# Messages' second pass of a graph layer: source rows gathered by index for seven of nine slot tiles

## The chip, the cores and the metric

The kernel runs on one core of a Trainium2 chip. A core has five engines that work side by side, each through its own queue in order: TensorE (PE, matrix products into PSUM; its weight loads are shown as PEld), VectorE (DVE), ScalarE (ACT), GpSimd (POOL) and SyncE (SP). DMAs move data between memory (HBM) and the on-chip SBUF. SP and ACT issue plain DMAs, POOL issues indirect ones, which take a list of row numbers. The metric is the device time of one execution in microseconds (us), median of several.

## The reference, cut to what matters

Four graph layers, each followed by a mixture of experts, are applied to 3125 nodes of 256 features with 50000 edges. The change lies in the second graph layer:

```python
def _L1_gnn_ref(h, edge_indices, edge_attr, W1, b1, W2, b2, W_ih, b_ih, W_hh, b_hh):
    src, dst = edge_indices
    m_in = concatenate([h[src], h[dst], edge_attr], -1)   # 256 + 256 + 64
    msg = relu(m_in @ W1.T + b1) @ W2.T + b2
    agg = segment_sum(msg, src, N)                          # sums by SOURCE node
    return gru_cell(agg, h, W_ih, b_ih, W_hh, b_hh)
```

(Written here in short.) With W1 cut in three by its input, an edge's hidden row is relu(P[src] + Q[dst] + edge_attr W1c), where P = h W1a + b1 and Q = h W1b are tables with one row per node. The kernel sums the relu rows by source and multiplies by W2 afterwards, once per node, with a count of edges for b2.

## The kernel before, in words

Nodes lie in 25 tiles of 128 and in seven blocks: six of four tiles and one of one tile. `mpnn_buckets` works in two passes over the edges.

**Pass one** (from L1298) takes the 392 edge tiles of 128 edges in order of destination, 28 groups of 14. `prepare` (L1275) finishes a block of nodes from the layer before: it fetches expert results, adds, normalizes, transposes on PE and multiplies by W1b into the table `q_tab` in HBM, two tiles at a time, copied by ACT and written by SP. It is called when the next group's destinations reach a new block. Each group forms Q[dst] + edge_attr W1c by one product per tile (L1316), out of a few `q_tab` rows near the destination (`near_load`, issued by SP), ACT copies it to `mq_r`, a last column holds the source's place in its tile (L1311), and POOL scatters the 128 rows of each tile by index into `slot_r` (L603). `slot_r` has a bucket for each tile of source nodes, 18 slot tiles of 128 rows long (8 for the last).

**Pass two** (from L1320) walks the buckets. For each bucket, `mb_p` is P for its 128 nodes (products L1344, b1 added at L1346), cut into three bf16 parts whose sum is exact enough (`split3`). For each group of GB = 9 slot tiles: SP loads `r` (`mb_r`, 1.16 MB, three buffers); DVE makes the mask `eq` per tile from the last column (L1360); PE transposes the masks (L1365) and ACT casts them to bf16 (`hot`, L1366); PE multiplies `hot` with the three parts (L1372), which places P[src] at each edge's row; DVE adds `r` (L1373), ACT applies relu (L1374) into `f` (`mb_m`, two buffers); and PE sums rows by source with the mask (L1376) into `acc`. After the four buckets of a block, `block` is the GRU cell (L984 and around), and `router.block` of the block before stands after the first bucket.

Tiles come from pools with a number of buffers; a buffer is free again when the last reader is done. The order of each engine's queue is laid down before the run by a planner: it walks the program with times of its own, takes of the instructions whose inputs it believes ready the one that stands first in the program, and so pulls later work forward where it sees an engine idle, as far as buffers allow. At run time each queue is strictly in order.

Of the kernel before, what the change touches and what calls it, by code (L numbers as in the profile page):

```python
# [8 lines left out]
F32 = mybir.dt.float32  # L9
# [8 lines left out]
P = 128  # L18
N = 3125
D = 256  # L20
# [75 lines left out]
def gnn_ffn_kernel(ctx: ExitStack, tc: tile.TileContext, I: dict, out: bass.AP):  # L96
# [1157 lines left out]
        def tile(self, shape, dtype, name):  # L1254
            return self.pool.tile(shape, dtype, name=self.name)

    def mpnn_buckets(pos, slot_r, collect, weights, router):

        with tc.tile_pool(name="mq", bufs=1) as p, tc.tile_pool(name="mq_t", bufs=1) as tp, \
                tc.tile_pool(name="mq_ps", bufs=2, space=PSUM) as pbt:
            q_tab = tc.dram_tile([NR, D], F32, name="mq_q")
            lane = p.tile([P, 1], F32, name="mq_l")
            V.tensor_scalar(lane, node_id[:, 0:1], 64.0, None, op0=OP.subtract)

            near = [p.tile([P, len(QUADS), D], F32, name=f"mq_n{k}") for k in range(4)]
            for t in near:
                for k in range(len(QUADS)):
                    nc.scalar.dma_start(t[:64, k], I["L1_gnn_W1T_c"])  # L1270
            w1b = load_w(p, "L1_gnn_W1T_b")
            add = add_two(x, weights)

            def prepare(s, n):
                t0, nt = s // P, n // P  # L1275
                for u0 in range(0, nt, 2):
                    m = min(2, nt - u0)
                    g = collect(tp, t0 + u0, m, 2)
                    for u in range(m):
                        add(t0 + u0 + u, g[:, :, u])  # L1280
                norm_tiles(tp, x, xn, t0, nt)
                xT = block_transposed(tp, pbt, xn, t0, nt, "mq_xT")
                for t in range(0, nt, 2):
                    m = min(2, nt - t)
                    pt = pbt.tile([P, 512], F32, name="bt_p")
                    for v in range(m):
                        for c in range(2):
                            PE.matmul(pt[:, v * D:(v + 1) * D], xT[:, c, (t + v) * P:(t + v + 1) * P], w1b[:, c],
                                      start=c == 0, stop=c == 1)
                    pv = pt[:, :m * D].rearrange("p (t d) -> p t d", d=D)  # L1290
                    o = tp.tile([P, 2, D], F32, name="mq_o", bufs=2)[:, :m]
                    S.copy(o, pv)
                    nc.sync.dma_start(node_rows(q_tab)[:, t0 + t:t0 + t + m], o)

            blocks = list(BLOCKS)
            put = scatter(slot_r, ET)
            with tc.tile_pool(name="mq_e", bufs=2) as ep, tc.tile_pool(name="mq_p", bufs=4, space=PSUM) as ps:
                for g in range(ET // GF):  # L1298
                    ahead = W_TO[min(g + 1, ET // GF - 1)]
                    while blocks and blocks[0][0] < ahead * P:  # L1300
                        prepare(*blocks.pop(0))

                    ea = ep.tile([P, GF * P], F32, name="mq_ea")
                    nc.sync.dma_start(ea[:64], I["edge_attrT"][:, g * GF * P:(g + 1) * GF * P])
                    row = ep.tile([P, GF * P], BF16, name="n_row")
                    nc.sync.dma_start(row[64:], near_row[g:g + 1].to_broadcast([64, GF * P]))
                    V.tensor_scalar(ea[64:], row[64:], lane[64:], None, op0=OP.is_equal)
                    for k in range(len(QUADS)):
                        near_load(g, k, near[g % 4][64:, k], q_tab, 1)
                    r = ep.tile([P, GF, D + 1], F32, name="mq_r", bufs=3)  # L1310
                    V.tensor_copy(r[:, :, D], sloc[:, g * GF:(g + 1) * GF])  # L1311
                    for u in range(0, GF, 2):
                        pt = ps.tile([P, 2, D], F32, name="mq_pe")
                        for v in range(2):
                            i = g * GF + u + v
                            PE.matmul(pt[:, v], ea[:, (u + v) * P:(u + v + 1) * P], near[g % 4][:, (u + v) // 4],  # L1316
                                      start=True, stop=True)
                        S.copy(r[:, u:u + 2, :D], pt)
                        for v in range(2):
                            i = g * GF + u + v  # L1320
                            put(pos[:, i:i + 1], r[:, u + v])
        with tc.tile_pool(name="mb", bufs=1) as p, tc.tile_pool(name="mb_e", bufs=2) as ep, \
# [3 lines left out]
                tc.tile_pool(name="mb_pp", bufs=2, space=PSUM) as ppp, \  # L1326
                tc.tile_pool(name="gru_ps", bufs=2, space=PSUM) as gps, \
                tc.tile_pool(name="gru_pt", bufs=1, space=PSUM) as gpt:
            w1a = load_w(p, "L1_gnn_W1T_a")
            b1 = load_bc(p, "L1_gnn_b1", D)  # L1330
            block, routed = gru(p), []
            for s, n in BLOCKS:
                hT = bp.tile([P, 2, 512], F32, name="mb_hT")
                for c in range(2):
# [4 lines left out]
                seg = bp.tile([P, 4, W], F32, name="mb_seg")  # L1339
                for u in range(n // P):  # L1340
                    b = s // P + u
                    pp = ppp.tile([P, 2, D], F32, name="mb_pp")
                    for c in range(2):
                        PE.matmul(pp[:, 0], hT[:, c, u * P:(u + 1) * P], w1a[:, c], start=c == 0, stop=c == 1)  # L1344
                    po = bp.tile([P, D], F32, name="mb_p")
                    V.tensor_tensor(po, pp[:, 0], b1, op=OP.add)  # L1346
                    parts = bp.tile([P, 3, D], BF16, name="mb_parts")
                    split3(bp, parts.unsqueeze(1), po.unsqueeze(1))
                    acc = pacc.tile([P, 512], F32, name="mb_acc")
                    for k0 in range(0, B_TILES[b], GB):  # L1350
                        m = min(GB, B_TILES[b] - k0)
                        r = ep.tile([P, GB, D + 1], F32, name="mb_r", bufs=3)
                        row = (b * BT + k0) * P
                        nc.sync.dma_start(r[:, :m], slot_r[row:row + m * P].rearrange("(k p) w -> p k w", p=P))
                        eq = ep.tile([P, GB, P], F32, name="mb_eq")
                        hot = ep.tile([P, GB, P], BF16, name="mb_hot")
                        f = ep.tile([P, GB, W], F32, name="mb_m")
                        V.memset(f[:, :m, D:], 1.0)
                        for k in range(m):
                            V.tensor_scalar(eq[:, k], iota1, r[:, k, D:], None, op0=OP.is_equal)  # L1360
                        for h0 in range(0, m, 4):
                            h1 = min(h0 + 4, m)
                            pt = ppt.tile([P, 512], F32, name="mb_tp")
                            for k in range(h0, h1):
                                PE.transpose(pt[:, (k - h0) * P:(k - h0 + 1) * P], eq[:, k], ident)  # L1365
                            S.copy(hot[:, h0:h1], pt[:, :(h1 - h0) * P].rearrange("p (k j) -> p k j", j=P))  # L1366
                        for h0 in range(0, m, 2):
                            h1 = min(h0 + 2, m)
                            pp = ppp.tile([P, 2, D], F32, name="mb_pp")
                            for k in range(h0, h1):  # L1370
                                for z in range(3):
                                    PE.matmul(pp[:, k - h0], hot[:, k], parts[:, z], start=z == 0, stop=z == 2)  # L1372
                            V.tensor_tensor(f[:, h0:h1, :D], r[:, h0:h1, :D], pp[:, :h1 - h0], op=OP.add)  # L1373
                            S.activation(f[:, h0:h1, :D], f[:, h0:h1, :D], AF.Relu)  # L1374
                        for k in range(m):
                            PE.matmul(acc[:, :W], eq[:, k], f[:, k], start=k0 + k == 0, stop=k0 + k == B_TILES[b] - 1)  # L1376
                    S.copy(seg[:, u], acc[:, :W])
                    if routed:
                        router.block(gp, Shared(gp, "segT"), Shared(gpt, "gru_t"), *routed.pop())
# [873 lines left out]
    with tc.If(in_windows == 1) as branch:  # L2253
        slot_r = tc.dram_tile([B_ROWS + 2 * P, D + 1], F32, name="slot_r")
        hy_sums = tc.dram_tile([NR + P, D + 1], F32, name="hy_sums")
        with tc.tile_pool(name="m1", bufs=1) as rp:
            router = Router(rp, 32, 1, "L1_ffn_router_wT", "L1_ffn_router_b")
            with tc.tile_pool(name="bk", bufs=1) as p:
                pos = p.tile([P, ET], I32, name="bk_i")
                with tc.tile_pool(name="m0", bufs=1) as mp:  # L2260
                    with tc.tile_pool(name="bk_t", bufs=1) as tp:
                        collect, weights = gat_gelu(mp, slot_r, hy_sums, bucket_slots(tp, pos))
                    mpnn_buckets(pos, slot_r, collect, weights, router)
            collect = top1_experts(router.hot)
        h_tab = tc.dram_tile([NR, D], F32, name="hc_tabc1")
        hyper_bn(h_tab, hy_sums, collect)
# [105 lines left out]
```

## Time and profile before

| what | value |
|---|---|
| median of the runs | 5283.61 us (5283.53 to 5300.94, 3 runs) |
| profiled execution | 5289.04 us, its span 5287.3 us |
| pass one, first to last scatter on POOL | 901 to 1445 us |
| pass two, from the first load of `r` to the last block's GRU | 1447 to about 2165 us |
| PE / DVE / ACT / POOL busy over the span | 73% / 46% / 23% / 43% |

The profile is one execution. "Busy" leaves out waits and the issuing of DMAs. A group row gives line, engine, operation, output<-inputs, shape, count, then busy us, mean ns of one, and idle time before it with what ended it. A timeline row begins with start and length in us. Matmul records of one fp32 product come in pairs, so counts at such lines are twice the products.

### The profile page before, as it was taken

The numbers are of one execution on the slowest core, as the hardware profiler recorded it, in microseconds if no ns is written. First come the engines' busy times: TensorE is split into PE (matmuls) and PEld (weight loads), VectorE is DVE, ScalarE is ACT, GpSimd is POOL, SyncE is SP. The second block draws the span as 40 slices with busy tenths as digits, with TensorE's granted clock in tenths as the row PEclk, the third lists the DMA queues.
The fourth block names the chain that finished last, engine by engine and source line by source line (L and its number), as shares of the span: only waits on it lengthen the run. The fifth ranks groups of instructions, "written<-read, shape, count | busy, mean of one in ns | idle before, by whom it ended". The sixth has DMA issues, their size and how long they took to land. (4 is left out here: it accounts for less than half of the span.)

```text
span 5287.3 us, 55222 instructions
## 1 busy us (share of the span) xinstructions
PE 3846.2 (73%) x16260; PEld 2652.4 (50%) x16260; DVE 2432.2 (46%) x9200; ACT 1239.1 (23%) x2517; POOL 2296.0 (43%) x2426
## 2 busy tenths in 40 slices
PE   4687647545399999445788888888888788875794
PEld 3466536434266666323555545556454444543583
DVE  6687746111055555456666556542333213336224
ACT  2010112212133333122344344343000200002121
POOL 3777454776700000227433343101777447771421
PEclk7788778767699999676888888888788668885797
DMA  6955256545432321265533443213333223331463
GB/s 195 296 157 157 91 180 211 162 154 160 146 100 86 91 90 62 64 201 145 139 99 106 115 114 96 56 51 114 105 105 105 68 81 104 105 105 32 167 216 131
DMA packets 391473, 655.82 MB, mean 124 GB/s; under 512 B 58519, under 2 KB 298330, under 8 KB 386810
## 3 DMA queue, kind: packets, MB, share of 16 engines
q1 hardware_dynamic: 266352, 339.40, 21.1%
q0 software_dynamic: 113712, 305.42, 19.4%
q10 hardware_dynamic: 11098, 7.31, 0.5%
q8 instruction: 140, 2.29, 0.2%
q14 instruction: 171, 1.40, 0.1%
HBM read 505.27 MB, written 146.64 MB: 123 GB/s over the span
## 5 line engine op out<-in xcount | busy, mean ns | idle before, releaser
L264 POOL DMA_INDIRECT hc_wm<-hc_tabc,src_col x784 | 748.1, 954 | 586.6 <-DMA a_L_gnn_c_b_col<-in_L_gnn_c_b_col 239.9
L348 PE MATMUL w_acc<-hc_wm,w_eq 128*128 128x256 f32 x2208 | 761.4, 474 | 191.7 <-DMA hc_wm<-hc_tabc,src_col 129.5
L348 PEld LDWEIGHTS w_acc<-hc_wm,w_eq 128*128 128x128 f32 x2208 | 447.7, 227 | 505.8 <-DVE w_eq L341 229.6
L341 DVE TENSOR_SCALAR w_eq<-iota,dloc,ew 128x128 f32<-128x128 f32 (+1 forms) x784 | 299.6, 384 | 750.3 <-PE w_acc L348 742.4
L264 POOL DMA_INDIRECT hb_r<-hy_x,src_col x392 | 380.7, 971 | 587.5 <-PE hb_acc L2026 304.3
L603 POOL DMA_INDIRECT slot_x<-xn,sl_i x125 | 121.5, 972 | 963.9 <-issue 832.3
L603 POOL DMA_INDIRECT slot_r<-mq_r,bk_i x392 | 396.2, 1011 | 181.4 <-issue 86.7
L264 POOL DMA_INDIRECT gw_m<-gat_h,src_col x392 | 402.4, 1027 | 133.7 <-issue 121.2
L1174 PE MATMUL gw_acc<-gw_m,gw_eqt 128*128 128x264 f32 x1104 | 310.6, 442 | 120.1 <-issue 87.5
L1316 PE MATMUL mq_pe<-mq_n,mq_ea 128*128 128x256 f32 x784 | 226.6, 460 | 210.6 <-issue 137.1
L1174 PEld LDWEIGHTS gw_acc<-gw_m,gw_eqt 128*128 128x128 f32 x1104 | 235.3, 219 | 182.4 <-issue 92.3
L603 POOL DMA_INDIRECT rows_y<-se_y,se_to x175 | 180.0, 1029 | 320.3 <-DVE se_y L696 186.1
L1316 PEld LDWEIGHTS mq_pe<-mq_n,mq_ea 128*128 128x128 f32 x784 | 183.8, 238 | 253.2 <-issue 198.2
L2026 PE MATMUL hb_acc<-hb_r,hb_eq 128*128 128x257 f32 x784 | 257.5, 459 | 54.3 <-DVE hb_eq L2023 45.9
L2056 PE MATMUL hb_pc<-n_near,n_hot 126*128 126x257 bf16 x392 | 123.9, 325 | 201.8 <-DVE hbe_a L2060 137.8
L1905 ACT ACTIVATE hb_h<-hb_ph,hb_o,hb_s 128x512 f32<-128x512 f32 (+2 forms) x256 | 172.9, 681 | 318.0 <-PE hb_ph L1903 317.7
L2026 PEld LDWEIGHTS hb_acc<-hb_r,hb_eq 128*128 128x128 f32 x784 | 170.7, 232 | 132.5 <-DVE hb_eq L2023 65.9
L683 ACT ACTIVATE se_h<-se_ph,se_w 128x256 f32<-128x256 f32 (+1 forms) x243 | 110.4, 455 | 494.7 <-PE se_ph L680 343.8
L2169 ACT COPY hc_seg<-w_acc 128x256 f32<-128x256 f32 x50 | 18.6, 372 | 874.4 <-PE w_acc L348 846.5
L680 PE MATMUL se_ph<-se_xT,se_w 128*128 128x256 f32 (+1 forms) x972 | 219.1, 370 | 3.7 <-DMA se_w<-in_L_ffn_lanes 1.4
L1903 PE MATMUL hb_ph<-hb_xT,hb_w 128*128 128x512 f32 (+2 forms) x512 | 212.7, 548 | 9.5 <-ACT hb_h L1905 9.1
L689 PE MATMUL se_py<-se_w,se_h 128*128 128x256 f32 x886 | 214.1, 384 | 2.3 <-ACT se_h L683 1.9
(543 smaller groups left out, 7073.9 us busy)
## 6 DMA issues: line engine op xcount, KB each, us to landing
mb_r<-slot_r SPq DMA_DIRECT2D x48, 1156.5 KB
se_w<-in_L_ffn_lanes SPq DMA_DIRECT2D x34, 1026.0 KB
hb_w<-in_L_ffn_W SPq DMA_DIRECT2D x128, 256.0 KB
w_row<-in_dst_row SPq DMA_DIRECT2D x28, 896.0 KB
se_r<-slot_x SPq DMA_DIRECT2D x66, 257.0 KB
se_w<-in_L_ffn_lanes SPq DMA_DIRECT2D x32, 513.0 KB
hb_w<-in_L_ffn_Wo SPq DMA_DIRECT2D x64, 256.0 KB
mq_ea<-in_edge_attrT SPq DMA_DIRECT2D x28, 448.0 KB
```

The lines of the kernel that those rows point to most:

```text
L264: nc.gpsimd.indirect_dma_start(out=dst, out_offset=None, in_=table, in_offset=bass.IndirectOffsetOnAxis(ap=idx, axis=0))
L341: V.tensor_scalar(eq[:, :n], iota256[:, :n], dloc[:, i:i + 1], scale[:, u:u + 1], op0=OP.is_equal, op1=OP.mult)
L348: PE.matmul(acc[t][:, :width], eq[:, k * P:(k + 1) * P], m[:, u, :width], start=i == W_FIRST[t], stop=i == W_LAST[t])
L603: d = nc.gpsimd.indirect_dma_start(out=table, in_=rows, in_offset=None, out_offset=bass.IndirectOffsetOnAxis(ap=idx, axis=0)).ins
L680: PE.matmul(ph, w[:, c, :P] if f < P else w[:, c * f + j * P:c * f + (j + 1) * P], xT[:, c], start=c == 0, stop=c == 1)
L689: PE.matmul(py[:, u], h[:, j, u * P:(u + 1) * P], w[:, :, P:2 * P] if f < P else w[:, o2 + j * D:o2 + (j + 1) * D], start=j == 0, stop=j = ...
L1174: PE.matmul(acc[t][:, :W], eq[:, k * P:(k + 1) * P], m[:, u], start=False, stop=i == W_LAST[t])
L1316: PE.matmul(pt[:, v], ea[:, (u + v) * P:(u + v + 1) * P], near[g % 4][:, (u + v) // 4], start=True, stop=True)
L1903: PE.matmul(ph[:, :n], ws[e, i][:, k, j * P:(j + 1) * P], src[:, k, :n], start=k == 0, stop=k == 1)
L1905: S.activation(o[:, j, :n], ph[:, :n], AF.Relu, bias=shift[i][:, e, j:j + 1], scale=scale[i][:, e, j:j + 1])
L2026: PE.matmul(acc[0][:, :D + 1], eq, b[:, u], start=u == 0, stop=u == GF - 1)
L2056: PE.matmul(pc[:, :D + 1], hot[:, u * P:(u + 1) * P], near[:, u // 4], start=True, stop=True)
```

## The change

`prepare` in pass one also multiplies the block by W1a, DVE adds b1, and SP writes the result into a second table `p_tab` (`mq_p`) in HBM. In pass two, a helper `fetch` loads `r` of a group, turns its last column into row numbers `ix` on DVE (`mb_ix`; place + 128 b - 1, at least 0) and has POOL gather the rows of `p_tab` by index straight into `f` for the first 7 of 9 tiles (6 of 8 in the last group). `fetch` of the next group stands in the program at the head of each group. The masks are still made for all nine tiles. Transposes, `hot` and products with the parts remain for the last two tiles only, which are added and passed through relu first; for the gathered ones DVE adds `r` and `f` in place, two tiles at a time. `mb_p` is read from `p_tab` instead of computed. `f` gets three buffers.

```diff
-    def mpnn_buckets(pos, slot_r, collect, weights, router):
+    def mpnn_buckets(pos, slot_r, collect, weights, router, p_tab):
...
             w1b = load_w(p, "L1_gnn_W1T_b")
+            w1a = load_w(p, "L1_gnn_W1T_a")
+            b1 = load_bc(p, "L1_gnn_b1", D)
...
                 for t in range(0, nt, 2):
                     m = min(2, nt - t)
-                    pt = pbt.tile([P, 512], F32, name="bt_p")
-                    for v in range(m):
-                        for c in range(2):
-                            PE.matmul(pt[:, v * D:(v + 1) * D], xT[:, c, (t + v) * P:(t + v + 1) * P], w1b[:, c],
-                                      start=c == 0, stop=c == 1)
-                    pv = pt[:, :m * D].rearrange("p (t d) -> p t d", d=D)
-                    o = tp.tile([P, 2, D], F32, name="mq_o", bufs=2)[:, :m]
-                    S.copy(o, pv)
-                    nc.sync.dma_start(node_rows(q_tab)[:, t0 + t:t0 + t + m], o)
+                    for w, tab in ((w1b, q_tab), (w1a, p_tab)):
+                        pt = pbt.tile([P, 512], F32, name="bt_p")
+                        for v in range(m):
+                            for c in range(2):
+                                PE.matmul(pt[:, v * D:(v + 1) * D], xT[:, c, (t + v) * P:(t + v + 1) * P], w[:, c],
+                                          start=c == 0, stop=c == 1)
+                        pv = pt[:, :m * D].rearrange("p (t d) -> p t d", d=D)
+                        o = tp.tile([P, 2, D], F32, name="mq_o", bufs=4)[:, :m]
+                        if w is w1b:
+                            S.copy(o, pv)
+                        else:
+                            V.tensor_tensor(o, pv, b1.unsqueeze(1).to_broadcast([P, m, D]), op=OP.add)
+                        nc.sync.dma_start(node_rows(tab)[:, t0 + t:t0 + t + m], o)
...
-            w1a = load_w(p, "L1_gnn_W1T_a")
-            b1 = load_bc(p, "L1_gnn_b1", D)
             block, routed = gru(p), []
+
+            def fetch(b, k0):
+                m = min(GB, B_TILES[b] - k0)
+                r = ep.tile([P, GB, D + 1], F32, name="mb_r", bufs=3)
+                row = (b * BT + k0) * P
+                nc.sync.dma_start(r[:, :m], slot_r[row:row + m * P].rearrange("(k p) w -> p k w", p=P))
+                ix = ep.tile([P, GB], I32, name="mb_ix", bufs=3)
+                V.tensor_scalar(ix[:, :m], r[:, :m, D], float(b * P - 1), 0.0, op0=OP.add, op1=OP.max)
+                f = ep.tile([P, GB, W], F32, name="mb_m", bufs=3)
+                for k in range(m * 7 // 9):
+                    gather(f[:, k, :D], p_tab, ix[:, k:k + 1])
+                return m, r, f
+
+            groups_left = [(b, k0) for b in range(NT) for k0 in range(0, B_TILES[b], GB)]
+            ahead = [fetch(*groups_left.pop(0))]
...
-                    pp = ppp.tile([P, 2, D], F32, name="mb_pp")
-                    for c in range(2):
-                        PE.matmul(pp[:, 0], hT[:, c, u * P:(u + 1) * P], w1a[:, c], start=c == 0, stop=c == 1)
                     po = bp.tile([P, D], F32, name="mb_p")
-                    V.tensor_tensor(po, pp[:, 0], b1, op=OP.add)
+                    nc.sync.dma_start(po, p_tab[b * P:(b + 1) * P])
...
-                        m = min(GB, B_TILES[b] - k0)
-                        r = ep.tile([P, GB, D + 1], F32, name="mb_r", bufs=3)
-                        row = (b * BT + k0) * P
-                        nc.sync.dma_start(r[:, :m], slot_r[row:row + m * P].rearrange("(k p) w -> p k w", p=P))
+                        m, r, f = ahead.pop(0)
+                        ng = m * 7 // 9
+                        if groups_left:
+                            ahead.append(fetch(*groups_left.pop(0)))
                         eq = ep.tile([P, GB, P], F32, name="mb_eq")
-                        hot = ep.tile([P, GB, P], BF16, name="mb_hot")
-                        f = ep.tile([P, GB, W], F32, name="mb_m")
+                        hot = ep.tile([P, GB - GB * 7 // 9, P], BF16, name="mb_hot")
...
-                        for h0 in range(0, m, 4):
-                            h1 = min(h0 + 4, m)
-                            pt = ppt.tile([P, 512], F32, name="mb_tp")
-                            for k in range(h0, h1):
-                                PE.transpose(pt[:, (k - h0) * P:(k - h0 + 1) * P], eq[:, k], ident)
-                            S.copy(hot[:, h0:h1], pt[:, :(h1 - h0) * P].rearrange("p (k j) -> p k j", j=P))
-                        for h0 in range(0, m, 2):
-                            h1 = min(h0 + 2, m)
-                            pp = ppp.tile([P, 2, D], F32, name="mb_pp")
-                            for k in range(h0, h1):
-                                for z in range(3):
-                                    PE.matmul(pp[:, k - h0], hot[:, k], parts[:, z], start=z == 0, stop=z == 2)
-                            V.tensor_tensor(f[:, h0:h1, :D], r[:, h0:h1, :D], pp[:, :h1 - h0], op=OP.add)
+                        pt = ppt.tile([P, 512], F32, name="mb_tp")
+                        for k in range(ng, m):
+                            PE.transpose(pt[:, (k - ng) * P:(k - ng + 1) * P], eq[:, k], ident)
+                        S.copy(hot[:, :m - ng], pt[:, :(m - ng) * P].rearrange("p (k j) -> p k j", j=P))
+                        pp = ppp.tile([P, 2, D], F32, name="mb_pp")
+                        for k in range(ng, m):
+                            for z in range(3):
+                                PE.matmul(pp[:, k - ng], hot[:, k - ng], parts[:, z], start=z == 0, stop=z == 2)
+                        V.tensor_tensor(f[:, ng:m, :D], r[:, ng:m, :D], pp[:, :m - ng], op=OP.add)
+                        S.activation(f[:, ng:m, :D], f[:, ng:m, :D], AF.Relu)
+                        for h0 in range(0, ng, 2):
+                            h1 = min(h0 + 2, ng)
+                            V.tensor_tensor(f[:, h0:h1, :D], r[:, h0:h1, :D], f[:, h0:h1, :D], op=OP.add)
                             S.activation(f[:, h0:h1, :D], f[:, h0:h1, :D], AF.Relu)
```

More of the change, by code (lines that the diff above doesn't have):

```diff
@@ L2255, in gnn_ffn_kernel @@
         hy_sums = tc.dram_tile([NR + P, D + 1], F32, name="hy_sums")
+        p_tab = tc.dram_tile([NR, D], F32, name="mq_p")
         with tc.tile_pool(name="m1", bufs=1) as rp:
@@ L2262, in gnn_ffn_kernel @@
                         collect, weights = gat_gelu(mp, slot_r, hy_sums, bucket_slots(tp, pos))
-                    mpnn_buckets(pos, slot_r, collect, weights, router)
+                    mpnn_buckets(pos, slot_r, collect, weights, router, p_tab)
             collect = top1_experts(router.hot)
```

## The prediction

> **What bounds the kernel now.** I read the page, then busy time by stage: columns are the engines' busy us (instructions), TensorE's granted clock, DMA share, GB/s.
>
> ```profile
> 901.00:1445.00 544.00, 254.02 (x901) 204.44 (x899) 66.23 (x159) 125.60 (x223) 395.91 (x392) 0.71 0.50 157
> 1533.00:1573.00 40.00, 37.09 (x122) 17.64 (x119) 16.35 (x37) 9.83 (x17) 0.00 (x0) 0.96 0.06 20
> 1573.00:1646.00 73.00, 69.65 (x442) 57.27 (x442) 45.61 (x162) 33.69 (x66) 0.00 (x0) 1.00 0.40 121
> 1646.00:1686.00 40.00, 37.09 (x121) 17.87 (x120) 16.38 (x38) 9.86 (x17) 0.00 (x0) 0.96 0.05 18
> 1686.00:2097.00 411.00, 389.04 (x2122) 282.66 (x2122) 231.07 (x747) 164.18 (x311) 0.00 (x0) 0.99 0.28 87
> 4300.00:4400.00 100.00, 81.51 (x233) 45.70 (x232) 33.32 (x84) 3.23 (x7) 75.94 (x80) 0.81 0.36 105
> ```
>
> Row 1 is pass one: POOL scatters 392 times in 544 us, 1.27 us each (0.97 plus 0.30 of issue), nearly without pause. Rows 2 to 5 are pass two: PE is busy 95%, POOL idle. Its rhythm: eight groups of nine tiles take 73 us, then the GRU holds PE for 40; from the last `mb_acc` matmul of a block to that of the next is 112.8 us (1532.9 to 2096.7 in the timeline is five). Row 6 is the later gather stage: 80 gathers of 1 KB rows per 100 us. Pass two by group (busy us, mean ns | idle before):
>
> ```profile
> L1376 PE MATMUL mb_acc<-mb_m,mb_eq 128*128 128x264 f32 x880 | 214.5, 389 | 0.4
> L1372 PE MATMUL mb_pp<-mb_parts,mb_hot 128*128 128x256 bf16 x1320 | 180.7, 275 | 0.6
> L1365 PE MATMUL mb_tp<-ident,mb_eq 128*128 128x128 f32 x440 | 88.0, 288 | 33.8 <-ACT mb_hot L1366 28.8 <-DVE mb_eq L1360 3.9
> L1344 PE MATMUL mb_pp<-w_L_gnn_W1T_a,mb_hT 128*128 128x256 f32 x100 | 27.8, 392 | 0.0
> ```
>
> **What is removed.** 48 groups keep 2 of 9 tiles, the last 2 of 8: 342 of 440 tiles leave PE. Transposes 342 x 0.200 (88.0/440) = 68; products 342 x 3 x 0.137 = 141; L1344 goes to pass one, 28. PE keeps per group 18 x 0.244 = 4.4 for the sums, 0.8 and 0.4 for the kept tiles: **5.6 us** instead of 9.1. Were PE the only bound, 237 us would go. It won't be.
>
> **What is added: seven gathers a group on an empty POOL queue.** Nearest row, the gather stage:
>
> ```profile
> L264 POOL DMA_INDIRECT hc_wm<-hc_tabc,src_col x80 | 76.0, 950 | 24.4 <-issue 23.4 <-PE w_acc L348 0.6 <-PE hc_tp L2154 0.3
> ```
>
> 7 x 1.25 = 8.75 us a group, already more than PE's 5.6: POOL becomes the bound between GRUs. It may be slower still. The new add `f = r + f` has both inputs in SBUF (before, one was PSUM): three of 0.68 us and one of 0.42 a group. Two places show POOL beside such an add:
>
> ```profile
> 801.52 1.23 POOL L603 DMA_INDIRECT rows_y<-se_y,se_to  x1 [0.30 <-issue]
> 801.95 0.57 DVE L1243 TENSOR_TENSOR bk_pos<-bk_pos,bk_cum 128x392 f32<-128x392 f32 x1
> 4982.97 1.48 DVE L2225 TENSOR_TENSOR x<-x,b_L_ffn_beta 128x1280 f32<-128x1280 f32 x1
> 4983.33 1.95 POOL L603 DMA_INDIRECT rows_y<-se_y,se_to  x1 [2.90 <-DVE se_y L696]
> ```
>
> Against 0.97 undisturbed, an add of 0.57 costs 0.26, one of 1.48 costs 0.98: about its length less 0.3 to 0.5. So 3 x 0.38 + 0.12 = 1.25 a group, and P, POOL's time per group, is **10.0 us**. [...] The adds' whole 2.46 us gives P = 11.2. [...] But in the gather stage one w_eq `tensor_scalar` runs beside each gather and the pace stays 1.25, so I charge nothing for those and take the rows: P between 8.75 and 11.2, 10.0 taken.
>
> DMA: gathers 0.36 share at full pace, today's loads of `r` 0.28 in pass two: 0.64, not a bound. `po` now comes by 25 loads of 128 KB on SP, behind `r` loads that wait for a free buffer; it is needed only by the kept tiles, and 0.4 us of DVE (L1346) goes for it. `ix` adds 49 small DVE instructions, some 0.2 us each. ACT casts fewer tiles. None is near a bound.
>
> **What a group ahead gives.** Everything hangs on POOL working during the GRU. Three buffers each of `r`, `ix`, `f` allow it: `f` of the block's last group is free when its sums are done. DVE must reach the `ix` early; its queue shows how far the planner pulls work forward:
>
> ```profile
> 1645.90 0.12 DVE L1358 MEMSET mb_m<- 128x72 f32 x1 [2.92 <-PE mb_acc L1376]
> 1645.94 0.68 DVE L1360 TENSOR_SCALAR mb_eq<-iota,mb_r 128x128 f32<-128x128 f32 x3
> 1646.66 0.69 DVE L966 COPY segT<-gru_t 128x512 f32<-128x512 f32 x1
> 1671.95 0.75 DVE L997 SCALAR_TENSOR_TENSOR hn<-gru_p,a_L_gnn_b_hh_col,rz 128x512 f32<-128x512 f32 x1 [16.70 <-PE gru_p L984]
> ```
>
> The masks of the next block's second group are made before the GRU: pulled as far as two buffers reach. With three I take three groups gathered in the GRU's 40 us (3P = 30). The third `ix` waits on DVE for an `r` whose load starts only when the block's last adds are done (6.4 us for the first load, 1447.5 to 1453.9); placed too early it holds the GRU's copies behind it, and PE behind those, by up to that; I charge nothing, since DVE idles 16.7 us before L997 where it can stand. Then: first group summed after 5.5 us and its buffer free; five more groups at POOL's pace, 5P; after the last gather 2.75 us to land (603.09 to 605.84 in the first gather stage), add, relu and last sums 1.65: 4.4. Then the GRU gap, 40. PE is now about half idle in the five, as in pass one, where the clock was 0.71 and 256-column matmuls averaged 460 ns: hidden by POOL there, 2 us at the GRU's cold start. [...]
> Cycle: 5.5 + 5P + 4.4 + 40 + 2 = 51.9 + 5P; five save 5 x (60.9 - 5P) = 304.5 - 25P.
> First block: nothing is gathered ahead. `r` lands at 1453.9, so its last sum is at 1454.3 + 8P + 4.4 against 1532.9: 74.2 - 8P.
> Last group behind the sixth GRU: eight tiles, about 3 us less.
>
> **Pass one.** 100 more matmuls (27.8 us at full clock), 13 DVE adds of 0.68, 13 SP writes. Most hide behind POOL's queue of scatters. Where they don't is the preparation:
>
> ```profile
> 1185.12 2.19 PE L1022 MATMUL bt_p<-ident,xn 128*128 128x128 f32 x8 [28.75 <-DVE xn L219]
> 1201.15 0.97 POOL L603 DMA_INDIRECT slot_r<-mq_r,bk_i  x1 [19.87 <-ACT mq_r L1318]
> ```
>
> POOL starves 19.9 us while PE, ACT, SP and the near-row loads finish a block in turn. A pair's `p` product (2.5 us) now stands on PE before the second `q` pair, and SP holds that pair's `q` write behind the `p` write, which waits for DVE; the near-row loads wait behind both. The two PSUM buffers of `bt_p` are freed by that add too. DVE itself may stand behind L1311, which waits up to 18 us for a scatter. Three places are exposed (before the first scatter at 901, at 941, at 1181): 2.5 to 8 us each, 4.3 taken: **13 us** lost (0 to 60 if all seven blocks stall so).
>
> **Sum:** 304.5 - 25P + 74.2 - 8P + 3 - 13 = 368.7 - 33P; at P = 10.0 a gain of **39 us**. The profiled execution (5289.0: span 5287.3 and 1.7 around it) goes to 5250; the median 5283.6 lies 5.4 lower, so **5245**. [...] Undisturbed (8.75): 5204.
>
> **Rivals.**
> - *POOL never stops* (0.10). If the planner pulls the next block's sums into the GRU, buffers come free there: the 20 us or so POOL is idle per cycle shrink; 15 off each of five: 5170. Against: PE has no gaps in the GRU to pull into (37.1 of 40 busy).
> - *DVE's order* (0.15). If adds of the next block's first group stand before L966, the GRU's copies wait for a gather that ends P after the last: some 7 us a cycle, 35 in all: 5280. For: DVE works in order, and pass one shows such waits.
> - *Only one group ahead* (0.10). Then seven groups, not five, run at P after the GRU: 46.4 + 7P, 116 at 10.0: slower by 34, 5318; at 9.4 about 5291.
> [...]
> - *Pass one stalls at every block* (0.05): 47 more, 5292.
>
> **Numbers.** The forecast's own case has 0.50, 5204 to 5262. A measurement here tells 0.5%, 26 us. Faster: 0.46 of it and 0.10; same: 0.04, 0.15, half of one group ahead, pass one: 0.29; slower: 0.15. Range 5180 to 5312.
>
> **What would show it.** Gather groups of 7 about 10 us apart, single gathers near 1.4 beside the adds; three groups in each GRU; the block cycle near 102; PE below 70% with a lower clock in pass two; pass one some 13 us longer. Wrong if POOL's queue is empty in the GRU, if DVE's L966 waits on `mb_m` gathers, or if P is above 11.

## The result, and the profile after

The changed kernel takes 5263.27 us (median of six runs, 5239.76 to 5272.12) beside 5287.99 us before on the same chip: ratio 0.9941, 95% interval 0.9915 to 0.9967, about 25 us by the medians and 31 by the ratio. The prediction was 5245, its likeliest range 5204 to 5262, its whole range 5180 to 5312: the measured time lies just above the likeliest range, and the gain is 25 to 31 us where 39 was written. The profiled execution took 5262.60 us, its span 5260.9.

Busy time by stage after, with the columns of the table of before in the prediction (us, then busy us and instructions of PE, PEld, DVE, ACT and POOL; granted clock, DMA share, GB/s): pass one, then the first two GRUs with the groups between them, then four more blocks.

```profile
911.00:1469.00 558.00, 257.56 (x983) 211.05 (x981) 72.58 (x170) 126.53 (x221) 396.54 (x392) 0.71 0.50 157
1562.00:1604.00 42.00, 36.39 (x106) 17.76 (x107) 20.41 (x45) 13.44 (x23) 16.63 (x15) 0.92 0.24 75
1604.00:1662.00 58.00, 44.06 (x211) 33.25 (x210) 38.52 (x152) 20.26 (x40) 40.28 (x40) 0.94 0.77 239
1662.00:1704.00 42.00, 36.81 (x108) 17.75 (x107) 20.97 (x49) 14.04 (x25) 16.04 (x16) 0.92 0.27 84
1704.00:2070.00 366.00, 297.07 (x1177) 193.95 (x1175) 221.80 (x755) 125.40 (x237) 214.33 (x208) 0.91 0.56 176
```

Between GRUs POOL is the busy one now: 40.28 us of gathers in 58, and 0.30 of issue between them. PE has fallen from 95% to 76% there. In the GRU POOL is busy gathering for some 16 us and then stops. The DMA share is 0.77 where gathers and loads of `r` meet, not the 0.64 that was added up. The groups of pass two:

```profile
L264 POOL DMA_INDIRECT mb_m<-mq_p,mb_ix x342 | 353.1, 1033 | 249.4 <-DVE mb_eq L1376 124.3 <-issue 86.0 <-DVE mb_m L1374 28.4
L1392 PE MATMUL mb_acc<-mb_m,mb_eq 128*128 128x264 f32 x880 | 257.7, 432 | 74.0 <-ACT mb_m L1390 54.9 <-ACT mb_m L1386 18.9
L1384 PE MATMUL mb_pp<-mb_parts,mb_hot 128*128 128x256 bf16 x294 | 44.4, 287 | 10.3 <-ACT mb_hot L1380 10.0
L1379 PE MATMUL mb_tp<-ident,mb_eq 128*128 128x128 f32 x98 | 20.8, 289 | 9.3 <-issue 7.4 <-DVE mb_eq L1376 1.8
```

Products and transposes went from 180.7 + 88.0 to 44.4 + 20.8 us. L1392, the same sums as L1376 before, grew from 214.5 to 257.7 us and from no idle time to 74.0: it waits for ACT's relu, ACT for DVE's add (L1390 behind L1389: 193.1 us in 96 waits), DVE for the gather to land (L1389: 173.2 us in 85).

From the timeline (last sum of each block): 1560.9, 1662.4, 1765.7, 1868.3, 1968.6, 2069.9, a cycle of **101.8 us** where 101.9 was forecast. From the end of pass one to the end of the last GRU's gates it is 665.8 us; before it was 714.4: 48.5 gained. Pass one gave back 24.1: its last scatter ends at 1469.4, not 1445.3. Of this 9.8 came ahead of the first scatter and 14.3 behind it. Net 24.4; the span fell by 26.4.

The queue that was to be watched, at the second GRU. `segT`, `degT` and `agg` are the GRU's copies; L1389 adds to gathered rows of the *next* block:

```profile
1663.86 0.68 DVE L966 COPY segT<-gru_t 128x512 f32<-128x512 f32 x1
1666.98 1.04 DVE L1389 TENSOR_TENSOR mb_m<-mb_r,mb_m 128x512 f32<-128x512 f32 x2 [2.45 <-DMA mb_m<-mq_p,mb_ix]
1668.03 0.62 DVE L966 COPY segT<-gru_t 128x512 f32<-128x512 f32 x1
1674.42 0.69 DVE L1389 TENSOR_TENSOR mb_m<-mb_r,mb_m 128x512 f32<-128x512 f32 x1 [2.09 <-DMA mb_m<-mq_p,mb_ix]
1675.03 0.68 DVE L978 COPY agg<-gru_p 128x512 f32<-128x512 f32 x1
```

The second `segT` copy and the first `agg` copy each come directly behind an add that waits for a gather, 2.45 and 2.09 us; the copies after them queue behind. All five cycles have such a wait ahead of the last `agg` copy. So the rival about DVE's order happened too, and with it one of the prediction's own signs of being wrong (L966 behind `mb_m` gathers). And pass one, where POOL's first long stop is, before and after:

```profile
943.76 0.97 POOL L603 DMA_INDIRECT slot_r<-mq_r,bk_i  x1 [3.15 <-ACT mq_r L1318]
```

```profile
937.03 3.77 PE L1291 MATMUL bt_p<-w_L_gnn_W1T_a,mq_xT 128*128 128x256 f32 x8 [9.26 <-DVE mq_o L1298]
949.76 0.18 DVE L1317 COPY mq_r<-sloc 128x14 f32<-128x14 f32 x1 [11.90 <-DMA slot_r<-mq_r,bk_i]
949.86 0.69 DVE L1298 TENSOR_TENSOR mq_o<-bt_p,b_L_gnn_b 128x512 f32<-128x512 f32 x1
950.61 1.11 PE L1022 MATMUL bt_p<-ident,xn 128*128 128x128 f32 x4 [9.37 <-DVE mq_o L1298]
958.37 0.97 POOL L603 DMA_INDIRECT slot_r<-mq_r,bk_i  x1 [10.40 <-ACT mq_r L1324]
```

Read the second block of rows upwards: POOL waits 10.40 us; PE stood still because DVE's add of b1 had not freed `bt_p`; and DVE's add stood behind L1317, which waits for a scatter.

### The profile page after: what moved, and what is told of

It reads as the page before. It is cut to its first block, busy times and chain, and to the rows that moved or that the text cites. A ratio compares the mean times of both kernels' runs of the same rounds, so it can differ in the third digit from the quotient of the medians.

```text
span 5260.9 us, 53356 instructions
## 1 busy us (share of the span) xinstructions
PE 3703.9 (70%) x14892; PEld 2525.3 (48%) x14892; DVE 2431.1 (46%) x9237; ACT 1188.7 (23%) x2420; POOL 2654.2 (50%) x2768
## 5 line engine op out<-in xcount | busy, mean ns | idle before, releaser
L348 PE MATMUL w_acc<-hc_wm,w_eq 128*128 128x256 f32 x2208 | 748.3, 467 | 204.9 <-DMA hc_wm<-hc_tabc,src_col 144.2
L348 PEld LDWEIGHTS w_acc<-hc_wm,w_eq 128*128 128x128 f32 x2208 | 441.1, 224 | 511.9 <-DVE w_eq L341 254.3
L264 POOL DMA_INDIRECT mb_m<-mq_p,mb_ix x342 | 353.1, 1033 | 249.4 <-DVE mb_eq L1376 124.3
L1322 PE MATMUL mq_pe<-mq_n,mq_ea 128*128 128x256 f32 x784 | 205.8, 429 | 153.8 <-issue 126.1
L1392 PE MATMUL mb_acc<-mb_m,mb_eq 128*128 128x264 f32 x880 | 257.7, 432 | 74.0 <-ACT mb_m L1390 54.9
L1322 PEld LDWEIGHTS mq_pe<-mq_n,mq_ea 128*128 128x128 f32 x784 | 170.4, 220 | 188.9 <-issue 156.9
L1392 PEld LDWEIGHTS mb_acc<-mb_m,mb_eq 128*128 128x128 f32 x880 | 173.1, 212 | 120.6 <-ACT mb_m L1390 67.0
L1919 PE MATMUL hb_ph<-hb_xT,hb_w 128*128 128x512 f32 (+2 forms) x512 | 214.5, 553 | 10.2 <-ACT hb_h L1921 10.1
```

Source lines behind the costliest of these rows:

```text
L264: nc.gpsimd.indirect_dma_start(out=dst, out_offset=None, in_=table, in_offset=bass.IndirectOffsetOnAxis(ap=idx, axis=0))
L348: PE.matmul(acc[t][:, :width], eq[:, k * P:(k + 1) * P], m[:, u, :width], start=i == W_FIRST[t], stop=i == W_LAST[t])
L1919: PE.matmul(ph[:, :n], ws[e, i][:, k, j * P:(j + 1) * P], src[:, k, :n], start=k == 0, stop=k == 1)
```

## The experiments

My theory going in: **POOL's pace between GRUs, and how many groups the buffers let it gather in a GRU, set the cycle.** Rivals: PE is still the bound; DVE's order at the GRU sets it; the adds hold POOL up for their whole length. A cycle is the time from the last sum of one block to that of the next; cycles below are means of five.

**The first four** ran on a chip where the kernel before took 5979.11 us and the granted clock in the profiles was 0.74 to 0.75; PE's idle time put down to issue at one line of a later stage (`w_acc`, L348) is 258.0 us in 75 stretches in the profile of the fourth, 7.0 us in one stretch in the profile of the changed kernel above. The changed kernel itself was not run on this chip, so the four are read against each other, not against 5263.

*Two buffers.*

```diff
-                r = ep.tile([P, GB, D + 1], F32, name="mb_r", bufs=3)
+                r = ep.tile([P, GB, D + 1], F32, name="mb_r", bufs=2)
...
-                f = ep.tile([P, GB, W], F32, name="mb_m", bufs=3)
+                f = ep.tile([P, GB, W], F32, name="mb_m", bufs=2)
```

> The changed kernel with two buffers instead of three of r, ix and f. If POOL's pace between GRUs and the number of buffers set the cycle, one group less is gathered in each GRU and stands behind it at P = 9.3 us: the cycle goes from 101.8 to about 111, five cycles give 47 us, 5310 in all. If the GRU's own waits or PE's order set the cycle instead, the time stays within some 10 us of 5263.

Measured: 6008.87 us, 1.0042 of before (1.0025 to 1.0058). Two groups are gathered in each GRU, as written; cycle 116.4. Without the kernel with three buffers on this chip that settles nothing yet; two buffers come back below.

*Six and eight tiles gathered* (6 or 8 for 7 in each `m * 7 // 9`).

> The changed kernel with six of nine tiles gathered instead of seven (the three kept tiles are multiplied two and one at a time). POOL as bound: P goes from 9.3 to 8.0, over 5 x 5 groups in the cycles and 8 in the first block 33 x 1.3 = 43 us less, about 5220; the cycle near 95. PE as bound: one more tile per group costs 0.2 + 0.4 us and some, 49 x 0.6 = 30 us more, 5293.

> The changed kernel with eight of nine tiles gathered. POOL as bound: P = 10.6, 33 x 1.3 = 43 us more, about 5306, cycle near 108. PE as bound: 30 us less, 5233.

Measured: six 5964.59 us, 0.9988 (0.9968 to 1.0008), cycle 109.0; eight 6085.45 us, 1.0195 (1.0178 to 1.0212), cycle 127.8. Eight costs 121 us more than six. Fewer gathers are faster: that is the sign for POOL as bound; for PE as bound it would be the other way round.

*Adds from PSUM.*

```diff
-                            V.tensor_tensor(f[:, h0:h1, :D], r[:, h0:h1, :D], f[:, h0:h1, :D], op=OP.add)
+                            V.tensor_tensor(f[:, h0:h1, :D], pp[:, :h1 - h0], f[:, h0:h1, :D], op=OP.add)
```

> The changed kernel, but each add of the gathered tiles takes the PSUM tile of the kept tiles' products as its second input instead of r from SBUF; its length on DVE stays near 0.68 us. The r rows of the gathered tiles are left out of the sums. If adds with two SBUF inputs hold POOL up, single gathers beside them fall from 1.13 to about 0.95 us; P falls from 9.3 to about 8.8, 33 x 0.5 = 16 us less, 5247. If they do not, gathers keep 1.13 beside the adds and the time stays within 5 us of 5263.

Measured: 6014.78 us, 1.0081 (1.0060 to 1.0101), cycle 119.2. The gain of 16 us that was written does not show: on the same chip two buffers have 116.4. An add now also needs the kept tiles' products, and POOL stops for up to 7.5 us between groups (seen in two cycles); that the one makes the other was not shown. The trace settles the durations all the same. A group of PSUM adds and the gathers beside it:

```profile
1941.84 2.21 DVE L1389 TENSOR_TENSOR mb_m<-mb_pp,mb_m 128x512 f32<-128x512 f32 x4
1942.96 0.95 POOL L264 DMA_INDIRECT mb_m<-mq_p,mb_ix  x1 [0.30 <-issue]
```

and the changed kernel beside two adds with both inputs in SBUF:

```profile
1645.43 1.28 DVE L1389 TENSOR_TENSOR mb_m<-mb_r,mb_m 128x512 f32<-128x512 f32 x2
1646.11 1.43 POOL L264 DMA_INDIRECT mb_m<-mq_p,mb_ix  x1 [0.30 <-issue]
```

Over the whole of pass two, taking every gather that overlaps an add by more than 0.05 us: 107 beside a PSUM add have mean 946 ns, 159 beside a two-SBUF add 1110 ns, 80 beside nothing on DVE 947. On the chip of this experiment, too, gathers beside two-SBUF adds took 1174 (six tiles) and 1134 (eight). So the second SBUF input holds gathers up, by 159 x 0.163 = 26 us over 49 groups: **0.53 us a group**. Were the whole length of the adds lost, it would be 2.46 (three of 0.68 us and one of 0.42). The mean hides two kinds: the median of the 159 is 949 ns, so half lose nothing, while the five longest, each beside two to four adds in a row, take 2.67 to 3.27 us, longer than 947 ns by 1.7 to 2.3 us where the adds cover 1.35 to 2.02 us of them. Eight gathers make up 12 of the 26 us. Gathers beside nothing but `mb_eq` masks took 956 ns (10 of them), so those cost nearly nothing.

**The next four** ran on a chip where before took 5291.61 us.

*P not made at all.*

```diff
-                    gather(f[:, k, :D], p_tab, ix[:, k:k + 1])
+                    gather(f[:, k, :D], q_tab, ix[:, k:k + 1])
```

with `prepare` as it was before the change and `mb_p` loaded from `q_tab`.

> Pass two as changed, pass one as before: the table of P is not made at all, and pass two gathers its rows, and loads its 128-row pieces, from the table of Q, which pass one makes anyhow (so the sums take Q's rows where P's belong). If making P is what pass one lost, its last scatter ends 24 us earlier in relation to its first, the first scatter comes 10 us earlier, and the whole is 24 us below the changed kernel, 5239. If pass one became longer for another reason, it stays at 5263.

Measured: 5289.14 us, 0.9998 (0.9983 to 1.0012), not the 5239 that was written. Other numbers come out of the layer, so the experts behind it get other rows, and the total can't be used; the stages up to there can. First to last scatter: 544.4 us, as before the change (544.0); 558.3 with P. The cycle is 101.5. So making P costs **13.9 us** inside pass one. The first scatter comes at 905.3 here; in the eight profiles on chips of that pace that make P it came at 903.3 to 911.1. The 9.8 us ahead of pass one in the profile after are therefore not the change's alone, and perhaps not due to it at all.

*P in another order and on other engines.*

```diff
-                for t in range(0, nt, 2):
-                    m = min(2, nt - t)
-                    for w, tab in ((w1b, q_tab), (w1a, p_tab)):
+                for w, tab in ((w1b, q_tab), (w1a, p_tab)):
+                    for t in range(0, nt, 2):
+                        m = min(2, nt - t)
...
+                            if w is w1a:
+                                PE.matmul(pt[:, v * D:(v + 1) * D], one, b1, start=False, stop=True)
...
-                        if w is w1b:
-                            S.copy(o, pv)
-                        else:
-                            V.tensor_tensor(o, pv, b1.unsqueeze(1).to_broadcast([P, m, D]), op=OP.add)
-                        nc.sync.dma_start(node_rows(tab)[:, t0 + t:t0 + t + m], o)
+                        S.copy(o, pv)
+                        (nc.sync if w is w1b else nc.scalar).dma_start(node_rows(tab)[:, t0 + t:t0 + t + m], o)
```

> The changed kernel with P made in another order in pass one: all products by W1b of a block and their writes stand before those by W1a; b1 is added by one more small product on PE, ACT copies the result, and ACT's queue writes it, so neither DVE nor SP has any part in it. If DVE's add behind a waiting copy and SP's queue are what pass one lost, nearly all of the 24 us come back: 5243. If it is PE's added products, it stays near 5263.

Measured: 5232.8 us, 0.9895 (0.9863 to 0.9928). Pass one takes 529.7 us, which is 28.6 less than with the change and 14.3 less than *before* it. The stop of 10.4 us is 3.2 again. The stop behind the 210th scatter, 19.9 us before and 22.9 after the change, is gone, and that I had not expected. DVE's queue shows why. Before:

```profile
1173.53 0.18 DVE L216 BATCH_NORM_AGGREGATE ln_mv<-ln_st 128x2 f32<-128x6 f32 x1
1183.11 0.18 DVE L1311 COPY mq_r<-sloc 128x14 f32<-128x14 f32 x1 [9.40 <-DMA slot_r<-mq_r,bk_i]
1184.65 1.38 DVE L219 TENSOR_SCALAR xn<-x,ln_mv,ln_rs 128x256 f32<-128x256 f32 x4
```

and in this experiment:

```profile
1155.51 0.18 DVE L208 RECIPROCAL ln_rs<-ln_e 128x4 f32<-128x4 f32 x1
1169.61 0.18 DVE L1320 COPY mq_r<-sloc 128x14 f32<-128x14 f32 x1 [13.92 <-DMA slot_r<-mq_r,bk_i]
1169.70 1.42 DVE L219 TENSOR_SCALAR xn<-x,ln_mv,ln_rs 128x256 f32<-128x256 f32 x4
```

The normalization of that block is waiting behind the same kind of copy (it waits for a scatter to free `mq_r`), but one group earlier, at a point where POOL still has a dozen scatters ready. Before, the copy was released by POOL's last work, and all that follows on PE, ACT and SP was exposed. The planner had laid the queues out anew; this part of the gain was not aimed at. The order, the engines and the writing queue of P were changed together, so what each of them gives is not told apart.

*Adds held behind the GRU's copies.*

```diff
-                V.tensor_copy(agg[:, j, :n], pa[:, :n])
+                agg_done[:] = [V.tensor_copy(agg[:, j, :n], pa[:, :n]).ins.name]
...
-                            V.tensor_tensor(f[:, h0:h1, :D], r[:, h0:h1, :D], f[:, h0:h1, :D], op=OP.add)
+                            d = V.tensor_tensor(f[:, h0:h1, :D], r[:, h0:h1, :D], f[:, h0:h1, :D], op=OP.add).ins
+                            if 2 * u + k0 // GB < 3 and block.agg_done:
+                                tc.add_manual_dep(d, block.agg_done[0], ..., reason="behind the GRU's copies")
```

(an order for the planner, with no wait at run time).

> The changed kernel with one thing more: the adds of the three groups that are gathered during a GRU stand on DVE behind the GRU's agg copies. If adds that wait for gathers ahead of these copies make the GRU 34 us long instead of 29, it goes back to 29 to 30, and five cycles give some 20 us: 5243. The sums of these groups come later; if that is what then sets POOL's restart, the gain is lost or turns into a loss of up to 5 us a cycle, 5290.

Measured: 5225.69 us, 0.9868 (0.9809 to 0.9927; the interval just touches that of the change, 0.9915 to 0.9967, so the trace decides). Cycle 96.2, so 5.6 less; end of pass one to last GRU 633.7 us instead of 665.8. DVE at the second GRU:

```profile
1652.57 0.69 DVE L968 COPY segT<-gru_t 128x512 f32<-128x512 f32 x1
1655.86 0.67 DVE L972 COPY degT<-gru_t 8x512 f32<-8x512 f32 x1
1657.74 0.69 DVE L980 COPY agg<-gru_p 128x512 f32<-128x512 f32 x1 [1.21 <-PE gru_p L979]
1658.60 0.69 DVE L980 COPY agg<-gru_p 128x512 f32<-128x512 f32 x1 [0.17 <-PE gru_p L979]
1659.21 4.40 DVE L1392 TENSOR_TENSOR mb_m<-mb_r,mb_m 128x512 f32<-128x512 f32 x8
```

From the first `segT` copy to the second `agg` copy it takes 8.1 us (1651.14 to 1659.3) instead of 12.8 (1663.86 to 1676.6). The GRU's products end 28.7 us after they start, as before the change (28.8), instead of 34.0. Little was lost behind: the five groups take 46.5 us instead of 45.9.

*Four buffers.*

```diff
-                f = ep.tile([P, GB, W], F32, name="mb_m", bufs=3)
+                f = ep.tile([P, GB, W], F32, name="mb_m", bufs=4)
...
-            degT = q.tile([8, 512], F32, name="degT")
+            rz = q.tile([P, 4, 512], F32, name="rz")
+            degT = rz[:8, 3]
...
-            hn = q.tile([P, 2, 512], F32, name="hn")
-            nn = q.tile([P, 2, 512], F32, name="nn")
+            hn = segT
+            nn = rz
```

(`r` and `ix` four too; `hT`, `seg`, `mb_p` one each.)

> The changed kernel with four buffers of r, ix and f instead of three; room for them comes from the GRU, whose temporaries share tiles, and from single buffers of hT, seg and p. If POOL's pace and the buffers set the cycle, four groups are gathered in a GRU, and a cycle gets shorter by one group, 9.3 us: 47 us in all, 5216. If PE or the GRU's waits set it, the time stays within 10 us of 5263.

Measured: 5295.7 us, 1.0005 (0.9991 to 1.0020), cycle 110.1: slower than the change with three. Neither side of the expectation came. Four groups are gathered ahead, but more of their adds stand among the GRU's copies: its products start 7.1 to 9.3 us after the block's last sum in four cycles (2.1 to 3.1 before and with held adds) and last 36 us. The smaller number of `hT`, `seg` and `mb_p` buffers and the shared GRU tiles came with it; what they cost was not measured apart.

**The last four** (before: 5291.73 us) put two repairs together, P made in the other order (by PE and ACT) and the adds held behind the GRU's copies, so that buffers and split could be varied without the order in the way.

> Both repairs together on the changed kernel: in pass one the products by W1b first and P through PE, ACT and ACT's queue; in pass two the adds of the three groups gathered ahead held behind the GRU's agg copies. If each gain stands for itself, pass one takes some 530 us, pass two's cycle some 96 us, and the whole is 5226 (the held adds alone) less 27 of pass one: 5199. If they interfere, it is not below 5226.

> As the one before with two buffers of r, ix and f instead of three (and the adds of two groups held). If POOL's pace and the number of buffers set the cycle: two groups are gathered in each GRU, a cycle is one group, 9.3 us, longer, near 105 us, and the time is 5199 + 47 = 5246. If the GRU's waits or PE set it: no more than 10 us above the kernel with three.

> As the first of these with four buffers of r, ix and f (room from shared GRU temporaries; the adds of four groups held). If POOL's pace and the buffers set the cycle: a group less behind each GRU, a cycle near 87 us, 5199 - 46 = 5153. PE's own work in a cycle is some 8 x 5.6 + 37 = 82 us, so PE can't be the bound before that. If it stays at 5199 or more, something that stands between GRU and sums is.

> As the first of these with six of nine tiles gathered. POOL as bound: P falls from 9.3 to 8.0, a cycle from 96 to 90, 33 x 1.3 = 43 us less in all, 5156. PE as bound: its work per group goes from 5.6 to 6.8 us with the third kept tile's transposes and products, a cycle can't be shorter than 8 x 6.8 + 37 = 91; and if PE's queue behind the GRU sets it already, the cycle grows to 100 and more, 5220 and above.

Measured, with a cycle cut at landmarks of the timeline, mean of five, in us (last sum to end of the GRU's products; from there to POOL's restart; POOL's groups; last gather to last sum):

| kernel | time | ratio, 95% interval | cycle | GRU | restart | gathers | tail |
|---|---|---|---|---|---|---|---|
| the change, profiled above | 5263.27 | 0.9941 (0.9915 to 0.9967) | 101.8 | 37.2 | 11.2 | 45.9 | 7.4 |
| two buffers, repaired | 5275.19 | 0.9963 (0.9947 to 0.9979) | 109.3 | 29.6 | 9.1 | 65.0 | 5.6 |
| three buffers, repaired | 5194.82 | 0.9812 (0.9794 to 0.9830) | 95.4 | 31.2 | 10.4 | 46.1 | 7.7 |
| four buffers, repaired | 5209.53 | 0.9837 (0.9820 to 0.9853) | 97.6 | 32.8 | 14.8 | 36.6 | 13.4 |
| three, six of nine tiles | 5187.79 | 0.9800 (0.9783 to 0.9816) | 95.0 | 29.9 | 12.2 | 43.8 | 9.0 |

The two repairs add up: 5199 was written, 5194.82 came. Pass one takes 529.5 to 530.9 us in all four.

*Two* against three buffers costs 80 us, more than the 47 written: six groups take 65.0 us, 10.8 each instead of 9.2: POOL now stops before each, for 0.5 to 5.2 us in the second and third cycle, where with three buffers it does not stop within its five groups.

*Four* against three gains nothing. The group saved (46.1 to 36.6) comes back: 4.4 us in the restart, 5.7 in the tail, 1.6 at the GRU. This is no clean test of the buffers: at the second GRU of this kernel ACT's copy into the one `hT` waits until L1005 has read the old one (1666.55), PE's transposes for the kept tiles stand behind that copy, and the kept tiles' add comes 7.1 us after the GRU's products; with three buffers and two `hT` it is 1.9.

*Six of nine tiles* is 7 us faster (intervals overlap) where 43 were written: a group of six gathers takes 8.8 us (43.8/5), not 8.0, since POOL now waits between groups too (0.7 to 2.2 us, at three places in each of these two cycles).

The stretch from the end of the second GRU to the last sum of the block, in the kernel with three buffers, the one with four and the one with six tiles:

```profile
1653.20:1717.90 64.70, 53.68 (x246) 40.35 (x244) 43.76 (x164) 22.05 (x44) 41.89 (x42) 0.87 0.71 219
```

```profile
1663.60:1728.80 65.20, 51.01 (x246) 38.88 (x245) 44.35 (x163) 21.66 (x42) 38.84 (x40) 0.92 0.68 211
```

```profile
1650.00:1716.40 66.40, 56.13 (x278) 43.40 (x277) 47.02 (x171) 24.55 (x48) 38.48 (x37) 0.90 0.66 202
```

65 us in all three, whatever POOL has left to do. PE is busy 51 to 56 of it in many short pieces (the router, the GRU's last transposes, kept tiles), at a clock of 0.87 to 0.92, DVE 44 to 47. So my theory holds on one side only: take work or a buffer away from POOL's advance and the cycle grows as its pace says or more; give it more and little or nothing comes. Work on PE and DVE behind a GRU that needs about as long is the likely reason, but what sets the 65 us was not told apart: PE, DVE, or, in their first 10 to 15 us, the load of `r` that POOL's restart waits for (shown below).

Both repairs with six of nine tiles are the best version run: 5187.79 us, 2.0% below the kernel before.

## Why the prediction was right, and where its terms were off

**The mechanism** stood. POOL became the bound between GRUs, three groups are gathered in each GRU, the cycle is 101.8 us against 101.9, PE fell from 95% to 76% with the clock at 0.91 to 0.94. Pass two gained 48.5 us where the steps give 51.7: five cycles 54.7 (54.5 written), the first block -3.9 (-5.8), behind the sixth GRU -2.3 (+3).

**The cycle's agreement is partly luck.** Written: 40 + 2 + 5.5 to POOL's restart, 50 for five groups, 4.4 behind them. Measured: 48.4, 45.9, 7.4.

- P, POOL's time per group, is 9.2 us (45.9/5), not 10.0. The term that was off is what an add costs: 1.25 us a group was taken from two rows in other stages, 0.53 measured. The adds' whole length makes 11.2 of P, none of it 8.75; the measured 9.2 lies between, so neither holds for these gathers as a whole, and a value between them, as the trace's rows gave it, was the right choice.
- The restart hides two errors. Without the adds among the copies it is 42.2 (the mean with held adds), so 47.5 was too long by 5.3. Of this, the 2 us for a cold start were the author's estimate, and no run shows them: with both repairs the GRU's products last 28.7 us in the mean of five, before 28.5, and the granted clock is 0.94 in the third GRU there (1717.9 to 1747.9) and 0.94 in the first two before (1535.3 to 1564.0, 1648.0 to 1677.0). And DVE's order, charged at nothing in the likeliest case, costs 6.2. The rival had it at 7 a cycle and gave it 0.15: it should have been a term, not a rival. That two errors of this size cancelled is luck. "DVE idles 16.7 us before L997 where it can stand" looked at the third `ix`, which did no harm; what stood ahead of the copies were the adds.
- POOL's restart is also not set by the buffer of `f`. `r` is the late one: its buffer is freed by the add of the kept tiles (L1385), which comes only behind the GRU. At the first GRU (the mask that the last row names is no input of the gather; `ix` is):

```profile
1602.16 0.68 DVE L1385 TENSOR_TENSOR mb_m<-mb_r,mb_pp 128x512 f32<-128x512 f32 x1
1602.87 1.60 SPq L1342 DMA_DIRECT2D mb_r<-slot_r  x2
1608.61 0.17 DVE L1344 TENSOR_SCALAR mb_ix<-mb_r 128x9 int32<-128x9 f32 x1 [0.45 <-DMA mb_r<-slot_r]
1609.62 1.03 POOL L264 DMA_INDIRECT mb_m<-mq_p,mb_ix  x1 [26.72 <-DVE mb_eq L1376]
```

The first group's sums, which free `f`, end at 1604.7, 4.9 us before the gather. In all five cycles here, and in those with held adds and of the last four, the first gather follows `ix` by 0.9 to 1.3 us. "First group summed and its buffer free" named the wrong buffer. No run gave `r` more buffers than `f`, so what an earlier load would bring is open.
- The tail is 7.4, not 4.4. At the end of the second block the last gathered adds are done at 1658.8, but the kept tiles' add (L1385) stands on DVE behind pieces of the next bucket and comes at 1659.82, and the last four matmuls at 1661.21 wait for its relu. The step took the gathered tiles to be last.

**Pass one**: 13 us forecast, 14.3 measured between first and last scatter (41.6 instead of 28.0 in long stops). Of the three places named, 941 took 7.2 more and 1181 took 3.0 more (there the products by W1a stand on PE between the two pairs by W1b, as written). The third was wrong: it is at 1293 (3.4 more), and what happens before the first scatter varies by 8 us between runs. At 941 the mechanism named (DVE's add behind L1311, PE behind it through `bt_p`) is the one in the trace.

**The total** is 18 us above the forecast: 3 from pass two, 11 from pass one and what lies ahead of it in this profile, and the rest within what runs of this kernel vary (32 us).

## What to carry to other kernels

When work is pulled ahead into a stage with its own chain on an in-order engine, price the pulled instructions that *wait* where they stand, in front of that chain: here 6 us a cycle, and a mere order without a wait took it out. A gain forecast from one engine's pace ends where the rest of the cycle takes as long (65 us here), so work out that second bound before adding a buffer. And cut a cycle at landmarks; a sum that agrees can be made of terms that don't.

## What the runs showed of the hardware

- A DVE add with two SBUF inputs (0.68 us) slows indirect gathers beside it from 947 to 1110 ns on average, about a fifth of the adds' own length (26 us under 121 us of adds): half of them lose nothing (median 949), the five longest, beside two to four adds in a row, 1.7 to 2.3 us, at least as much as those adds last beside them (1.35 to 2.02). Beside an add with one input in PSUM they take 946 (107 of them, none over 949).
- One chip took 13% longer than the others for the same kernel, before the change (5979 against 5288 to 5292 us), with single instructions of the usual length and more idle time between them: in the profiles of the changed kernels the matmuls at L348 average 457 to 460 ns there and 461 to 473 elsewhere, the gathers `hc_wm` 951 to 953 and 955 to 957, and PE's idle time before L348 is 444 to 464 us and 196 to 218. Why was not looked into; on it the split showed its sign clearly, the number of buffers did not.
